# Similarity matmuls of two heads issued by turns on the two halves of TensorE's rows, in a fixed order

## The chip, the core and the metric

The kernel runs on one core of one Trainium2 chip. The time is device microseconds of one execution of the whole program. Three runs of the kernel before took 3486.24, 3478.69 and 3476.59 us; their median is 3478.69.

The names in the text: TensorE (PE in the profile; PEld is its loading of weights) multiplies matrices into PSUM banks, VectorE (DVE), ScalarE (ACT) and GpSimd (POOL) work on elements, SyncE (SP) issues the transfers. Each engine takes its instructions in the order in which they stand in its own queue.

## What is computed

The reference is a small transformer on x of 4 batch elements, 2048 tokens and 256 features, all in float32. Cut to what matters:

```python
x = x + LN(attention_ref(LN(x)))      # softmax(x x^T) over all tokens, times x
x = x + LN(ffn_ref(LN(x)))            # two layers, below

def layer(x):                          # DEPTH = 2, HEADS = 8, DIM_HEAD = 64, WINDOW = 128
    h = shift_token(x)
    q, k, v = split(h @ wqkv)          # to heads
    q, k = rotary_xpos(l2norm(q) * qs, l2norm(k) * ksc)
    # each window of 128 queries sees its own 128 keys and the 128 of the window before
    sim = einsum('bhwid,bhwjd->bhwij', q * 8, k);  mask
    o = softmax(sim) @ v
    x = x + o @ wo
    h = LN(shift_token(x)) @ w1 + b1
    a, g = split(h)
    return x + (a * gelu(g)) @ w2 + b2
```

## The kernel before

Tokens lie on the 128 partitions for the row statistics and the residual stream, features for the products. First comes the attention over all tokens, for each of four batch elements (the first 690 us or so). Then two layers run over 4 x 16 windows of 128 tokens each, 128 window steps in all, with one layer's weights held in SBUF.

**Products in two parts.** A float32 operand is kept as two float32r parts whose sum is exact (`Split`: hi and lo). A product is three matmuls into the same PSUM tile: lo times hi, hi times lo, hi times hi. They are written by the helper `products` (matmul on L149), so nearly all matmuls of the profile carry line 149 and are told apart by tile.

**Similarities (L696 on, function `similarities`).** A window step makes its similarities in two batches (gq 0 and 1) of four heads. A head has 64 features, so its matmul uses 64 of the array's 128 rows. Heads lie in pairs: of a pair, one head (r = 0) has its features on partitions 0 to 63, the other (r = 1) on 64 to 127. The heads of one r share a PSUM tile, `ps[r]`, in a bank of its own; the pair is c = 0 or 1. So a batch has 2 (c) x 2 (r) groups of three matmuls, each of 256 columns (the keys of two windows; 128 in the first window of a batch element). In the profile they are `sim<-kT_h,qT_l`, `sim<-kT_l,qT_h` and `sim<-kT_h,qT_h`.

**What reads them.** For each of the four heads VectorE adds the mask, scales, and finds the row's minimum (L702, `pr<-sim`, with `nm`, by a second small instruction on the same line); ScalarE takes the exponential and its sum (L707); VectorE inverts the four sums (L713, `rr`); GpSimd divides three of the four heads and ScalarE one (L720, L718). Then TensorE transposes (L730, `pp`), the two parts `pT` are made by ScalarE (L132) and VectorE (L137), and the values' matmuls (`po`) and the output's (`pw`) follow.

**Banks.** PSUM tiles come from tags with a fixed number of banks. The tag `sim` has two, shared by `sim`, `pa` (the first product of the feed-forward), `phn` (its transposed input) and `pv` (the values' projection):

```python
BANKS = {'sim': (2, ('sim', 'pa', 'phn', 'pv')), 'po': (3, ('po', 'pw')), 't75': (1, ('pf', 'ph', 'pqk')), ...}
```

**What sets the order.** The window steps' stages (queries and keys, softmax, outputs, feed-forward) are written down by turns after the strings in `TURNS`. What decides the order in each engine's queue is a scheduler: `schedule_with_timeline_sim=True` lets it place the instructions by a simulated time of its own, within what data and buffers allow. In the order that it made, 125 of the 256 batches have the six matmuls of r = 0 and the six of r = 1 as two blocks with other work between them, 121 have the two blocks one directly after the other, and ten (first windows) have other forms.

Of the kernel before, what the change touches and what calls it, by code (L numbers as in the profile page):

```python
# [14 lines left out]
P = 128  # L15
HEADS = 8
DH = 64
# [29 lines left out]
class Split:  # L47
    """A float32 operand in two float32r parts whose sum is exact: its upper 12 bits and the rest."""
# [9 lines left out]
def sandwich_kernel(  # L58
# [16 lines left out]
    """x += LN(attention over the batch's tokens of LN(x)); x += LN(two local-attention layers of LN(x)).  # L75

    First the attention over all tokens for each batch element, then each layer for all of them,
    with that layer's weights in SBUF. Tokens are on the partitions for the row statistics and the
    residual stream, features for the products, which are taken of operands in two parts each.
    """  # L80
    nc = tc.nc
# [3 lines left out]
    HID = w2.shape[1]  # L85
# [3 lines left out]
    NC = HID // P  # whole chunks of the hidden layer  # L89
    TAIL = HID - NC * P  # and the rest, the gate's at partition 64  # L90
    GT = 64
    # Where rows of the tail lie again: to, from, how many.
    PIECES = ((TAIL + 1, 0, GT - TAIL - 1), (GT + TAIL, GT - TAIL - 1, P - 1 - GT - TAIL))
    RING = 3  # windows whose keys and values are kept
# [6 lines left out]
    # ---------------------------------------------------------------- constants  # L101
# [6 lines left out]
    one = const.tile([P, 1], F32, name="one")  # L108
    nc.gpsimd.memset(one, 1.0)
    # Query i of a window sees keys i .. i + 128 of the previous and its own window: those of the  # L110
    # previous from i on, those of its own up to i. Here for the order previous, own, previous.
# [12 lines left out]
    # ---------------------------------------------------------------- operands in two parts  # L124
# [17 lines left out]
    def products(dst, terms, whole=()):  # L142
        """dst = the sum of the terms' lhsT.T @ rhs, with all of float32's bits, and of whole's as they are."""
        todo = []
        for a, b in terms:
            todo += [(a.lo, b.hi), (a.hi, b.lo), (a.hi, b.hi)]
        todo += whole
        for n, (a, b) in enumerate(todo):
            nc.tensor.matmul(dst, a, b, start=(n == 0), stop=(n == len(todo) - 1))  # L149

    # ---------------------------------------------------------------- row statistics
    def statistics(parts, n, name):
        """Mean and variance of n rows' parts, and 1/sqrt(variance + eps): [P, n, 2], [P, n]."""
        k = len(parts[0])
        mv = small.tile([P, 4, 2], F32, tag="mv", bufs=12, name=f"mv_{name}")
        for i in range(n):
            bs = small.tile([P, 2, 6], F32, tag="bs", name=f"bs_{name}_{i}")
            for c, part in enumerate(parts[i]):
                nc.vector.bn_stats(bs[:, c, :], part)
            nc.vector.bn_aggr(mv[:, i, :], bs[:, 0:k, :].rearrange("p c s -> p (c s)"))  # L160
        ve = small.tile([P, 4], F32, tag="ve", name=f"ve_{name}")
        nc.vector.tensor_scalar_add(ve[:, 0:n], mv[:, 0:n, 1], EPS)
        rstd = small.tile([P, 4], F32, tag="rstd", bufs=12, name=f"rstd_{name}")
        nc.gpsimd.tensor_tensor(rstd[:, 0:n], ve[:, 0:n], neghalf[:, 0:n], ALU.pow)
        return mv, rstd
# [6 lines left out]
    def normalize_all(dst, src, mv, rstd, engines, name):  # L172
        """Rows i of src, normalized, on the vector engine or the scalar engine."""
        n = len(src)
        if "a" in "".join(engines):
            mr = small.tile([P, 4], F32, tag="mr", name=f"mr_{name}")
            nc.vector.scalar_tensor_tensor(mr[:, 0:n], mv[:, 0:n, 0], -1.0, rstd[:, 0:n], ALU.mult, ALU.mult)
        for i in range(n):
            for d, s, e in zip(dst[i], src[i], engines[i]):
                if e == "a":  # L180
                    nc.scalar.activation(d, s, AF.Identity, bias=mr[:, i : i + 1], scale=rstd[:, i : i + 1])
                else:
                    normalize(d, s, mv, rstd, i)
# [10 lines left out]
    def add_context(xg, y, b, g):  # L194
        """x + LN(y) goes to DRAM, and y becomes LN of that."""
# [10 lines left out]
    # ---------------------------------------------------------------- attention over all tokens  # L206
    JG = 2

    def global_phase(early, res, keep, big, bank):
        """Attention over all tokens.  # L210

        It stops before the last group's scores, when it's done with early, and after them, when
        it's done with res; the rest, in steps, uses only keep and bank.
        """
# [3 lines left out]
        def slot(tag, n, last):  # L218
            """The pool and the tag for the n-th of a kind of tiles; last are those that the last group uses."""
            n, last = n % GB[tag], [i % GB[tag] for i in last]  # L220
            return (res if n in last else early), f"{tag}{n}"

        def load_x(b, g):
            pool, tag = slot("x", b * NG + g, [B * NG - 1])
            t = pool.tile([P, 4, D], F32, tag=tag, bufs=1, name=f"x_{b}_{g}")
            # The first to come is waited for.
# [6 lines left out]
        def prepare(b, g):  # L233
            """LN(x) of 512 tokens with the features on the partitions."""
            xg = xt[b, g]
            mv, rstd = statistics([[xg[:, s, :]] for s in range(4)], 4, f"x_{b}_{g}")
            # |LN(x_j)|^2, the shift of column j's exponents: the exponents are 64 at most, one is 0.
# [21 lines left out]
        def scores(b, jg, hf):  # L259
            """exp of a half of the rows of JG chunks of scores."""  # L260
# [12 lines left out]
            for j in range(jg * JG, (jg + 1) * JG):  # L273
# [6 lines left out]
                # The scores are symmetric: those of the groups before are transposed here.  # L280
# [27 lines left out]
            for j in range(jg * JG, (jg + 1) * JG):  # L308
                # The sums belong to the contraction's index, so they divide LN(x).
# [14 lines left out]
        def context(b, jg, hf):  # L324
            """Adds the context of JG chunks; at the end x + LN(context) and LN of that go to DRAM."""
            for g in (2 * hf, 2 * hf + 1):
# [19 lines left out]
                if jg == NW // JG - 1:  # L346
                    if b + 1 < B:
                        add_context(early.tile([P, 4, D], F32, tag="xr", bufs=GB["xr"], name=f"xr_{b}_{g}"), y, b, g)
                    # The last one's rest is done when the first layer takes it.
# [37 lines left out]
    # ---------------------------------------------------------------- weights of a layer  # L387
# [5 lines left out]
    def tables(early, pool, l):  # L393
        """Rotation tables with the scales of q and k; the halves are swapped as the rotation does."""
# [29 lines left out]
    # The weights' parts, as they lie in SBUF.  # L424
# [11 lines left out]
    def split_weights(pool, bank, l):  # L436
        """Leaves layer l's weights in two parts in DRAM, piece by piece; each is left half a turn to arrive."""
        # The scale of the layer norm goes into w1, its shift into the bias.
# [34 lines left out]
        for i, (kind, ks, cols, src) in enumerate(pieces):  # L473
# [14 lines left out]
            # The lower part takes raw's place.  # L488
# [18 lines left out]
        # The tail's parts and the bias's, which meet rows of ones, share the rows of one product.  # L507
# [13 lines left out]
    def load_weights(pool, w, l, kinds):  # L521
        """Layer l's weights into w, as soon as the ones before aren't used any more."""
# [8 lines left out]
    # ---------------------------------------------------------------- the layers  # L531
    def layer_phase(pool, bank, ending):
# [22 lines left out]
        def features(l, b, u):  # L555
            """h of windows 2u and 2u + 1, features on the partitions: the second half comes one token late."""
# [21 lines left out]
        def queries_keys(l, b, w, n, wt, own):  # L578
            """Queries, keys and values of window w, left in own; in stages."""
# [19 lines left out]
            # Rotation, with the decay, the scales and, for q, the factor -8 in the tables; l2norm.  # L599
# [46 lines left out]
            # The similarities are scaled by q's.  # L646
# [18 lines left out]
        def local_attention(l, b, w, wt, before, own):  # L665
            """Window w sees itself and the window before it; y += its attention. In two streams of stages."""
# [5 lines left out]
            else:  # L672
# [3 lines left out]
                # In the order of their slots.  # L676
# [7 lines left out]
            def similarities(gq):  # L684
                # Negated similarities; the two heads of a pair use the two halves of the array's
                # rows, and so two banks.
                ps = [bank(f"sim_{at}_{gq}_{r}").rearrange("p (c j) -> p c j", c=2) for r in range(2)]
                for c in range(2):
                    for r in range(2):
# [5 lines left out]
                        products(ps[r][:, c, 0:NK], [(qT[rows_, 2 * gq + c, :], keys)])  # L695
# [28 lines left out]
            def weights(m):  # L724
                """The weights of pair m with the keys on the partitions."""
# [8 lines left out]
            def values(m, pT, po):  # L734
                # Both heads' values against both heads' weights: the diagonal blocks count.
# [42 lines left out]
        def feed_forward(l, b, w0, m, wt):  # L778
            """y += FFN of m windows from w0 on, in stages; h2's first row is there already."""
# [3 lines left out]
            # The second half of the features, one token late.  # L783
# [34 lines left out]
            for n, c in enumerate((*range(TAILPOS), NC, *range(TAILPOS, NC))):  # L818
# [4 lines left out]
                # a * gelu(g) takes the place of a.  # L823
# [54 lines left out]
        def finish(b, w0, m, ys):  # L878
            """x += LN(y) of m windows."""
# [78 lines left out]
    class Pools:  # L958
        """The layers' memory: what the first steps use, to the left, and the rest, once the phase before is over."""
# [4 lines left out]
        def more(self, n):  # L964
            """The part of the phase before goes, what takes its place comes."""
# [46 lines left out]
def _rope(n, window):  # L1012
    """Rotation tables [cos or sin, n, q or k, DH / 2] with xpos's decay, and q's factor 8, negated."""
# [43 lines left out]
```

## Time and profile before

| | |
|---|---|
| median of three runs | 3478.69 us (3476.59 to 3486.24) |
| the profiled execution's span | 3480.2 us |
| granted TensorE clock, mean | 0.991 |
| TensorE matmuls, busy | 3374.0 us (97%), 24312 instructions |
| VectorE busy | 2932.9 us (84%) |
| ScalarE busy | 2495.6 us (72%) |
| GpSimd busy | 1933.8 us (56%) |
| similarity matmuls | 3 x 1024, of them 3 x 960 with 256 columns |

The profiled execution has no other time of its own than its span, which lies within the spread of the three runs. A matmul's length in the profile is from its start to its modelled end, and matmuls overlap: 256 columns are shown as some 280 ns while the next one starts some 120 ns after. So busy time of TensorE is more than the work it has room for, and the step from one start to the next is what a matmul costs. In the timeline a row with "x2" merges two instructions of one kind that overlap.

### The profile page before, as it was taken

How to read it: one execution, taken by the hardware profiler on the slowest of the kernel's cores; microseconds unless marked ns; L12 is line 12 of the kernel's file. 1: busy time of each engine (PE TensorE's matmuls, PEld its weight loads, DVE VectorE, ACT ScalarE, POOL GpSimd, SP SyncE). 2: the span in 40 equal slices, each digit the busy share in tenths (PEclk: the TensorE clock that was granted, in tenths of full speed). 3: DMA queues.
4: the chain of work that ended last, by engine and by line, in shares of the span. 5: the costliest groups of instructions: out<-in, count | busy, mean ns of one | idle time of the engine just before them, and what ended most of it. 6: DMA issues, size and time to landing. Idle time of an engine off the chain costs nothing.

```text
span 3480.2 us, 67843 instructions
## 1 busy us (share of the span) xinstructions
PE 3374.0 (97%) x24312; PEld 3069.6 (88%) x24312; DVE 2932.9 (84%) x7549; ACT 2495.6 (72%) x5826; POOL 1933.8 (56%) x1975
## 2 busy tenths in 40 slices
PE   8999999999999999999999999999999999999997
PEld 7989999978889999999888898888888888888886
DVE  6797877778888888888999888888888888888886
ACT  5556655467777888777777777777777777777774
POOL 3234313265556666666666655666666666566562
PEclk9999999999999999999999999999999999999998
DMA  3243312110000000001111112101000010011001
GB/s 98 93 145 116 127 47 92 63 65 22 23 23 25 24 25 23 23 25 34 36 35 35 49 59 68 29 29 30 29 29 29 29 31 25 26 30 30 29 22 30
DMA packets 158194, 156.70 MB, mean 45 GB/s; under 512 B 27466, under 2 KB 145056, under 8 KB 157344
## 3 DMA queue, kind: packets, MB, share of 16 engines
q1 hardware_dynamic: 157856, 152.36, 14.1%
q8 instruction: 192, 3.15, 0.4%
q14 instruction: 146, 1.20, 0.1%
HBM read 86.39 MB, written 54.79 MB: 41 GB/s over the span
## 4 chain that ended last, share of the span: by engine, by line
PE 79%; DVE 11%; ACT 5%; DMA 2%; issue 2%; POOL 1%; SPq 0%; POOLq 0%; ACTq 0%; DVEq 0%
PE pa L149 12%; PE sim L149 10%; PE po L149 9%; PE pqk L149 9%; PE c L149 8%; PE pf L149 6%; PE pp L730 6%; PE pv L149 5%; PE pw L149 5%; PE s L149 5%; PE pqkT L657 3%; DVE pr L702 2%; DVE hn L168 1%; DVE y L168 1%; DVE qk L648 1%
## 5 line engine op out<-in xcount | busy, mean ns | idle before, releaser
L720 POOL TENSOR_SCALAR pr<-pr,rr 128x256 f32<-128x256 f32 (+1 forms) x768 | 356.1, 481 | 650.9 <-DVE rr L713 494.2
L707 ACT ACTIVATE pr<-pr,nm 128x256 f32<-128x256 f32 (+1 forms) x1024 | 507.8, 498 | 123.4 <-DVE nm L702 118.5
L702 DVE CUSTOM_DVE_ANT_0 pr<-sim,mask,rn 128x256 f32<-128x256 f32 (+1 forms) x1024 | 440.1, 470 | 92.3 <-PE sim L149 88.5
L149 PE MATMUL pa<-hnT_h,w_l 128*128 128x256 f32 x1408 | 407.1, 289 | 3.5 <-DVE hnT_l L137 2.2
L630 POOL TENSOR_TENSOR rn<-ss,neghalf 128x16 f32<-128x16 f32 x128 | 394.1, 3079 | 27.7 <-DVE ss L610 20.0
L616 POOL TENSOR_TENSOR sw<-qk,ab 128x512 f32<-128x512 f32 x256 | 338.3, 1322 | 115.2 <-ACT qk L596 115.2
L149 PE MATMUL pa<-hnT_l,w_h 128*128 128x256 f32 x1408 | 398.8, 283 | 0.3 <-DVE hnT_l L137 0.2
L149 PE MATMUL pa<-hnT_h,w_h 128*128 128x256 f32 x1408 | 399.0, 283 | 0.0
L137 DVE TENSOR_TENSOR pT_l<-pp,pT_h 128x512 fp32r<-128x512 f32 (+1 forms) x512 | 340.0, 664 | 27.7 <-ACT pT_h L132 23.4
L623 POOL TENSOR_TENSOR qk<-qk,ab 128x512 f32<-128x512 f32 x256 | 349.4, 1377 | 10.2 <-ACT sq L602 9.0
L132 ACT CAST pT_h<-pp 128x512 fp32r<-128x512 f32 (+1 forms) x512 | 291.7, 570 | 68.2 <-PE pp L730 62.8
L149 PE MATMUL po<-pT_l,v_h 128*128 128x256 f32 x992 | 316.3, 319 | 4.6 <-DVE pT_l L137 4.6
L730 PE MATMUL pp<-ident,pr 128*128 128x128 f32 x1984 | 314.6, 276 | 3.7 <-DVE pT_l L137 1.7
L149 PE MATMUL po<-pT_h,v_l 128*128 128x256 f32 x992 | 298.2, 301 | 2.6 <-ACT pT_h L132 2.4
L132 ACT CAST act_h<-af 128x256 fp32r<-128x256 f32 x320 | 130.2, 407 | 237.2 <-DVE af L833 233.9
L149 PE MATMUL sim<-kT_h,qT_l 64*128 64x256 f32 (+1 forms) x1024 | 294.0, 329 | 0.9 <-ACT kT_h L132 0.6
L149 PE MATMUL c<-xs_h,e_l 128*128 128x256 f32 x1024 | 285.3, 285 | 3.6 <-ACT y L132 2.5
L149 PE MATMUL c<-xs_l,e_h 128*128 128x256 f32 x1024 | 287.5, 283 | 0.8 <-POOL xs_l L137 0.8
L149 PE MATMUL c<-xs_h,e_h 128*128 128x256 f32 x1024 | 287.5, 283 | 0.0
L149 PE MATMUL po<-pT_h,v_h 128*128 128x256 f32 x992 | 278.9, 281 | 0.0
L149 PEld LDWEIGHTS pa<-hnT_h,w_l 128*128 128x128 f32 x1408 | 269.4, 191 | 5.6 <-DVE hnT_l L137 2.7
L149 PEld LDWEIGHTS pa<-hnT_l,w_h 128*128 128x128 f32 x1408 | 269.5, 191 | 1.1 <-DVE hnT_l L137 1.0
(179 smaller groups left out, 11841.3 us busy)
## 6 DMA issues: line engine op xcount, KB each, us to landing
yd<-y SPq DMA_DIRECT2D x32, 512.0 KB
y<-yd SPq DMA_DIRECT2D x32, 512.0 KB
ab<-abd SPq DMA_DIRECT2D x128, 128.0 KB
x<-in_L_attn_x_dram SPq DMA_DIRECT2D x15, 512.0 KB
x<-x1d SPq DMA_DIRECT2D x15, 512.0 KB
out_dram<-y SPq DMA_DIRECT2D x15, 512.0 KB
h<-y SPq DMA_DIRECT2D x64, 112.0 KB
xr<-in_L_attn_x_dram SPq DMA_DIRECT2D x12, 512.0 KB
```

The costliest lines, as they stand in the source:

```text
L132: (nc.scalar.copy if eng == "a" else nc.vector.tensor_copy if eng == "v" else nc.gpsimd.tensor_copy)(dst, src)
L137: eng.tensor_tensor(dst.lo, src, dst.hi.bitcast(F32), ALU.subtract)
L149: nc.tensor.matmul(dst, a, b, start=(n == 0), stop=(n == len(todo) - 1))
L168: nc.vector.tensor_scalar(dst, src, mv[:, i, 0:1], rstd[:, i : i + 1], ALU.subtract, ALU.mult)
L616: nc.gpsimd.tensor_mul(sw4[:, hs], qk4[:, hs, ::-1, :], ab[:, 1, j].unsqueeze(1).to_broadcast([P, HEADS, 2, DH // 2]),)
L623: (nc.vector if T1[j] == "v" else nc.gpsimd).tensor_mul(qk[:, hs, :], qk[:, hs, :], ab[:, 0, j].rearrange("p h i -> p (h i)").unsqueeze(1) ...
L630: nc.gpsimd.tensor_tensor(rn, ss, neghalf, ALU.pow)
L657: nc.tensor.transpose(pt[:, c * P : (c + 1) * P], qk[:, j * HEADS + 2 * c : j * HEADS + 2 * c + 2, :].rearrange("p h d -> p (h d)"), ident,)
L702: nc.vector.tensor_tensor_reduce(out=pr[:, r, 0:NK], in0=sim, in1=mask[:, m0 : m0 + NK], scalar=3.0e38, scale=own["rn"][:, h : h + 1] if Q ...
L707: nc.scalar.activation(pr[:, r, 0:NK], pr[:, r, 0:NK], AF.Exp, bias=nms[h], scale=-1.0, accum_out=rs[:, h : h + 1],)
L720: (nc.gpsimd if e == "p" else nc.vector).tensor_scalar(pr, pr, rr[:, h : h + 1], 1.0, ALU.mult, ALU.mult)
L730: nc.tensor.transpose(pp[:, f, r, :], prs[m][:, r, f * P : (f + 1) * P], ident)
```

## The change

The four groups of a batch are no longer written one after the other. For each pair c, the three matmuls of r = 1 and the three of r = 0 are written by turns, beginning with r = 1, and a new helper ties each of the twelve to the one before it, without a semaphore (`NoSync`), so that the scheduler keeps them in that order on TensorE's queue. It may still put other instructions between them. The operands, the PSUM tiles and what reads them are the same; only comments and docstrings go besides, which moves the line numbers (`products`' matmul is L161 after, the similarities' own matmul L715).

```diff
+    def in_turn(instructions):
+        for a, b in zip(instructions, instructions[1:]):
+            tc.add_manual_dep(
+                b.ins, a.ins.name,
+                mybir.DependencyInfo(mybir.DependencyClass.NoSync, mybir.DependencyReason.DATA), reason="turns",
+            )
+
+    def terms_of(terms):
         todo = []
         for a, b in terms:
             todo += [(a.lo, b.hi), (a.hi, b.lo), (a.hi, b.hi)]
-        todo += whole
+        return todo
+
+    def products(dst, terms, whole=()):
+        todo = terms_of(terms) + list(whole)
         for n, (a, b) in enumerate(todo):
             nc.tensor.matmul(dst, a, b, start=(n == 0), stop=(n == len(todo) - 1))
...
                 ps = [bank(f"sim_{at}_{gq}_{r}").rearrange("p (c j) -> p c j", c=2) for r in range(2)]
+                queue = []
                 for c in range(2):
-                    for r in range(2):
+                    pair = []
+                    for r in (1, 0):
                         rows_ = slice(r * DH, (r + 1) * DH)
                         keys = Split(*(
                             t[rows_, first : first + (nh - 1) * step + 1 : step, 2 * gq + c, :]
                             for t in (kT.hi, kT.lo)
                         ))
-                        products(ps[r][:, c, 0:NK], [(qT[rows_, 2 * gq + c, :], keys)])
+                        pair.append((ps[r][:, c, 0:NK], terms_of([(qT[rows_, 2 * gq + c, :], keys)])))
+                    for n in range(3):
+                        for dst, todo in pair:
+                            queue.append(nc.tensor.matmul(dst, *todo[n], start=(n == 0), stop=(n == 2)))
+                in_turn(queue)
```

More of the change, by code (lines that the diff above doesn't have):

```diff
@@ L140, in move @@
         queue.dma_start(out=dst.bitcast(F32), in_=src.bitcast(F32) if src.dtype == F32R else src)
-    def products(dst, terms, whole=()):
+    def in_turn(instructions):
[5 more added lines that the diff above has]
+    def terms_of(terms):
         todo = []
```

## The prediction

> **What bounds the kernel now.** I read the page's busy times first, then its chain of work that ended last, then the busy time by stretches of the span, then the timeline of TensorE around the matmuls that the change touches, and last the waits.
>
> ```profile
> span 3480.2 us, 67843 instructions
> PE 3374.0 (97%) x24312; PEld 3069.6 (88%) x24312; DVE 2932.9 (84%) x7549; ACT 2495.6 (72%) x5826; POOL 1933.8 (56%) x1975
> PE 79%; DVE 11%; ACT 5%; DMA 2%; issue 2%; POOL 1%; SPq 0%; POOLq 0%; ACTq 0%; DVEq 0%
> ```
>
> TensorE is busy nearly always and carries 79% of the chain; VectorE is next with 84% and 11%. The stretches say how close VectorE is in the layers, which start at about 700 us:
>
> ```profile
> core 0: us, PE busy (x) PEld busy (x) DVE busy (x) ACT busy (x) POOL busy (x), PEclk, DMA share, GB/s
> 2100.00:2500.00 400.00, 387.81 (x2806) 350.57 (x2805) 350.11 (x924) 301.25 (x742) 248.60 (x258) 0.99 0.10 28
> ```
>
> In 400 us VectorE is idle for 50. A busy TensorE is not one at its peak, so I count steps from one matmul's start to the next. In the timeline (start, length, engine, line, operation) a matmul of 256 columns takes a step of 0.12 us although each is shown 0.28 long. Here is a half of a batch of similarities alone (six matmuls on 64 rows):
>
> ```profile
> 2000.14 0.28 PE L149 MATMUL po<-pT_l,v_h 128*128 128x256 f32 x1
> 2000.26 0.28 PE L149 MATMUL po<-pT_h,v_h 128*128 128x256 f32 x1
> 2000.47 0.38 PE L149 MATMUL sim<-kT_h,qT_l 64*128 64x256 f32 x1
> 2000.69 0.28 PE L149 MATMUL sim<-kT_l,qT_h 64*128 64x256 f32 x1
> 2000.81 0.28 PE L149 MATMUL sim<-kT_h,qT_h 64*128 64x256 f32 x1
> ...
> 2001.16 0.27 PE L149 MATMUL sim<-kT_h,qT_h 64*128 64x256 f32 x1
> 2001.37 0.38 PE L149 MATMUL pw<-wo_h,oT_l 128*128 128x256 f32 x1
> ```
>
> Entering costs a step of 0.21 instead of 0.12, the first step inside 0.22, leaving 0.21: the half takes 0.90 from its first start to the next kind's, and 0.99 with the 0.09 lost on entry. And here are two halves, the lower rows' six and then the upper rows' six, directly one after the other:
>
> ```profile
> 2006.89 0.38 PE L149 MATMUL sim<-kT_h,qT_l 64*128 64x256 f32 x1
> 2007.12 0.28 PE L149 MATMUL sim<-kT_l,qT_h 64*128 64x256 f32 x1
> 2007.23 0.28 PE L149 MATMUL sim<-kT_h,qT_h 64*128 64x256 f32 x1
> 2007.24 0.39 PE L149 MATMUL sim<-kT_h,qT_l 64*128 64x256 f32 x2
> 2007.46 0.29 PE L149 MATMUL sim<-kT_l,qT_h 64*128 64x256 f32 x2
> 2007.58 0.28 PE L149 MATMUL sim<-kT_h,qT_h 64*128 64x256 f32 x2
> 2007.70 0.28 PE L149 MATMUL sim<-kT_h,qT_l 64*128 64x256 f32 x1
> ...
> 2007.94 0.28 PE L149 MATMUL sim<-kT_h,qT_h 64*128 64x256 f32 x1
> 2008.15 0.66 PE L730 MATMUL pp<-ident,pr 128*128 128x128 f32 x4
> ```
>
> The rows with x2 are the point: two matmuls, one of each half, start within 0.01 us and the next pair follows 0.12 later. So the two halves of the array do run side by side here, but only three of six pairs: twelve matmuls take 1.26 us, 1.35 with the entry.
>
> **The change part by part.** *Order.* Each of the 256 batches (128 window steps, two each) has 12 similarity matmuls. In the order of the program before, 125 batches stand as two separate halves, 121 as twelve together (six more, of a first window with 128 columns, alternate by three already, and four have 2 and 10). In the changed program 141 stand as twelve alternating, 105 as one lone matmul of the upper rows, then other work, then the eleven others; the ten of first windows remain about as they were. No instruction is added or removed on any engine, and the 839 transfers of the SP queue are the same ones. The scheduler does shift everything else, on POOL's and SP's queues too; I give that no price beyond the waits below, as POOL idles 38% and the transfers use 10% of the DMA engines in the stretch shown.
>
> *TensorE's steps, removed.* Before: 125 x 2 x 0.99 = 247.5 and 121 x 1.35 = 163.4, together 410.9 us. After, if all six pairs run as the three x2 rows do: 0.22 + 4 x 0.12 + 0.21 + 0.09 on entry = 1.00 for a block. A lone matmul pays entry and exit for itself: 0.09 plus a step between 0.21 (an exit) and 0.31 (an exit and the slow first step), so 0.30 to 0.40; I take 0.35, between, as no row shows one. After: 141 x 1.00 + 105 x 1.35 = 282.8. That is 128 us less (123 to 133), all of it on the engine that carries the chain.
>
> *Waits, added.* PE's queue is in order, and less TensorE time now lies between a result and its use. For each matmul that waits for another engine I counted the TensorE steps between it and the last matmul that its data depend on. With under 2.5 us of cover there are 386 such waits before and 784 after. In the trace of before a wait with 1.5 to 2.5 us of cover costs about 0.1 us on average (mostly the next weight load, which comes late), one with 1.0 to 1.5 us about 0.25. Taking each class at its mean in before: about 40 us more. Ends: nothing, if VectorE simply idles less, and 80 us, if each of the 398 new ones cost 0.2. I take 45, a little over the middle, because VectorE has less idle time left to take them up.
>
> *The banks.* A batch now holds both banks of the tag sim until VectorE has read four tiles, 4 x (470 + 83 ns) = 2.2 us with line 702's two groups; pa, phn and pv use the same two banks. Before, VectorE could start on one half when its six were done; now its first reading waits for the whole batch, 0.9 us after the batch starts, as long as a half took alone. That is no loss where the twelve stand together. In the 105 split batches the lower rows' reading starts later by the work in between (some 2 to 4 us); the rows that use it, the transposes of L730, stand a median of 10 us behind in both orders, which covers it.
>
> *VectorE as the next limit.* Its work stays. Its waits for ScalarE in the layers (rr 60, af 40, and splits qT, pT, oT, ss, act, hT, kT of 13 to 25 each, in all 227 us of 2780) are 33 in 400 us, so 350 + 33 = 383 is a floor of about 17 us less per 400, or 118 us over the layers. The gain of 128 can't come through whole.
> The Trainium skill (TensorEngine Tiling (Array Packing), "PSUM Bottleneck") speaks against the change here: tiling makes TensorE faster, not the reading of PSUM, which may become the bottleneck. By this rule alone the sum would be the 118 us just worked out, or nothing if VectorE's idle time stayed at 50; by the matmul rows alone 128. No row before decides between them.
>
> *Sum.* 3480.2 - 128 + 45 = 3397; I say 3400. The sum is made against the profiled execution, whose span is 1.5 us over the median of the runs shown, 3478.69, less than their own spread of 10; 0.3% (10 us) is about what a measurement can tell from no change.
>
> **The rivals.** *A: VectorE takes over.* TensorE's steps go, but VectorE's idle time falls only from 50 to 45 in 400: 35 us gained, 3445. For it: VectorE's 88% in the layers and its waits for ScalarE. Against it: 88.5 us of its idle time are waits for the similarities themselves, and those ought to shrink.
>
> ```profile
> DVE pr L702 <- PE sim L149: 88.5, 142, 2.0
> PE phn L811 <- DVE nm L702: 30.8, 16, 2.4
> ```
>
> *B: slower, the bank wait.* The second line is TensorE standing until VectorE has read a batch out of a bank: 16 times, 1.93 us each. Both banks are now wanted at once, in a fixed order beginning with the upper rows, and all that follows in PE's queue stands behind that wait. Once 43 of the 256 batches pay 1.93 us (83 us, 128 less the 45), the gain is gone; at 60 it is 3513. Against it: the next matmul on a batch's bank stands a median of 2.8 us of steps after the batch (2.7 is what an end and four readings need), close, but at most places not short by a whole wait.
>
> *C: the change doesn't do what it says.* If the pairs don't keep up over six (loads of both halves getting in each other's way), a block costs 1.35 as now: 141 x 1.35 + 105 x 1.70 = 368.9, 42 us less, and with the 45 of waits 3483, no change. The x2 rows speak against it: the weight loads of both halves went side by side there too.
>
> *D: all of it.* Waits stay as they are: 3352.
>
> **How the numbers follow.** Forecast (3375 to 3435) 0.50; D (below 3375) 0.12; A (3435 to 3470) 0.20; C or a draw (3470 to 3490) 0.05; B (above 3490) 0.13. Faster 0.82, same 0.05, slower 0.13. The range is 3358 to 3472, leaving out about 0.05 below and 0.15 above.
>
> **What would show it.** Right: pairs of sim matmuls (x2) 0.12 us apart through whole blocks, about 0.9 us a block; a smaller share of sim in the chain; VectorE near 360 busy of 400. Wrong by A: a larger DVE share of the chain with idle TensorE spread over many short waits. Wrong by B: one group, PE sim, phn, pv or pa waiting for DVE nm, with 100 us and more. Wrong by C: rows of sim with x1.

## The result and the profile after

The changed kernel takes 3544.77 us, the median of four runs (3537.96 to 3546.88), against 3481.27 us for the kernel before (3476.59 to 3486.24): a ratio of 1.0178, with a 95% interval of 1.0163 to 1.0192. It is slower by 1.8%, where 3400 us and faster had been forecast. The profiled run took 3537.96 us with a span of 3536.2, that is 56 us more than the span before.

The page of the kernel after, its span, its busy times and its chain of work that ended last:

```profile
span 3536.2 us, 67828 instructions
PE 3321.2 (94%) x24312; PEld 2968.3 (84%) x24312; DVE 3029.2 (86%) x7549; ACT 2478.9 (70%) x5826; POOL 1918.2 (54%) x1975
PE 48%; DVE 29%; ACT 14%; DMA 3%; issue 3%; POOL 2%; SPq 1%; POOLq 0%; DVEq 0%; ACTq 0%
```

Three things differ from before. TensorE is busy for 53 us less, with the same 24312 matmuls, and yet the span is longer: so it stands idle for 109 us more (215 against 106). Its share of the chain fell from 79% to 48%, and VectorE's rose from 11% to 29%, ScalarE's from 5% to 14%. And VectorE is busy for 96 us more although it has the same 7549 instructions, which nothing in the change had asked for.

The same stretch as before, by its busy times:

```profile
core 0: us, PE busy (x) PEld busy (x) DVE busy (x) ACT busy (x) POOL busy (x), PEclk, DMA share, GB/s
2100.00:2500.00 400.00, 375.94 (x2787) 332.37 (x2786) 356.55 (x905) 294.02 (x737) 240.09 (x253) 0.99 0.13 41
```

VectorE went from 350 to 357 busy of 400, TensorE from 388 to 376. The granted clock of this stretch is the same 0.99.

Over the whole span the clock has a small share. The trace shows short episodes, mostly of 3.4 us, at half clock. In the kernel before one of them comes 1.4 us behind a TensorE wait of 2.4 us (phn for nm, ended at 2545.65); it and the 3.4 us behind it:

```profile
2547.00:2550.40 3.40, 3.40 (x9) 2.68 (x9) 3.34 (x9) 1.57 (x4) 2.27 (x1) 0.50 0.00 0
2551.00:2554.40 3.40, 3.40 (x31) 3.40 (x30) 2.29 (x4) 3.38 (x6) 3.40 (x6) 1.00 0.00 0
```

Inside, matmuls of 512 columns take steps of 0.43 us, just ahead of it 0.23. There are 13 such episodes before (61 us) and 19 after (82 us). TensorE's steps in the layers that fall into them take 19 us over the usual ones of their kind before and 29 after, so at most 10 of the 56 us are the clock's. What sets an episode off was not tested; 11 of the 13 and 17 of the 19 begin within 5 us of the end of a TensorE step longer than 1 us.

The change itself does what it says. The timeline of TensorE in the kernel after (start, length, engine, line, operation) shows a batch of twelve:

```profile
2011.72 0.28 PE L161 MATMUL pf<-w2t,tail 128*128 128x256 f32 x1
2011.93 0.38 PE L715 MATMUL sim<-kT_h,qT_l 64*128 64x256 f32 x2
2012.15 0.28 PE L715 MATMUL sim<-kT_l,qT_h 64*128 64x256 f32 x2
2012.27 0.28 PE L715 MATMUL sim<-kT_h,qT_h 64*128 64x256 f32 x2
2012.39 0.28 PE L715 MATMUL sim<-kT_h,qT_l 64*128 64x256 f32 x2
2012.51 0.28 PE L715 MATMUL sim<-kT_l,qT_h 64*128 64x256 f32 x2
2012.63 0.28 PE L715 MATMUL sim<-kT_h,qT_h 64*128 64x256 f32 x2
```

All six similarity rows are pairs (x2), 0.12 us apart after the slow first step. Over the whole trace such a block takes a median of 0.909 us from its first start to the next kind's (1.254 before). Where one matmul of the upper rows stands alone, it costs this:

```profile
2017.25 0.38 PE L715 MATMUL sim<-kT_h,qT_l 64*128 64x256 f32 x1
2017.56 0.50 PE L161 MATMUL pqk<-wq_h,hT_l 128*128 128x512 f32 x1
```

0.31 us from start to start, with the 0.09 lost on entry 0.40.

I added up all steps of TensorE in the layers (from 700 us on) from start to start, and split off what a step has over the usual one of its kind as a wait. Before: 2492 us of steps and 261 of waits. After: 2377 and 431. So 115 us of steps went, and 170 us of waits came: 55 more, which is the 56 of the span. (Steps slowed by the clock count as waits here. The split moves by some 15 us with what is called the usual step; the sum does not.) The waits are many and short: those over 0.35 us rose from some 80 or 90 to some 220. By the matmul that waits (count, us): phn 17 (41) to 52 (67), pp 7 (5) to 35 (34), po 8 (8.5) to 32 (27), pv 3 (3.5) to 19 (17), sim 2 (0.9) to 19 (17).

TensorE's larger waits in the kernel after (who waits, for whom, us in total, times, the longest in us):

```profile
PE pp L751 <- DVE pT_l L137: 27.9, 31, 2.3
PE phn L832 <- DVE nm L723: 27.4, 22, 2.9
PE po L161 <- ACT pT_h L132: 20.4, 32, 1.2
PE sim L715 <- DVE nm L723: 15.8, 21, 0.9
PE phn L832 <- ACT hn L193: 15.6, 12, 7.4
...
PE phn L832 <- DVE hn L180: 14.4, 18, 1.1
PE pqkT L669 <- DVE qk L657: 13.3, 17, 1.6
PE pv L161 <- DVE nm L723: 12.4, 16, 1.3
```

No single group carries the loss. Before, the phn wait for nm was the only one above 10 us. The waits of VectorE for the similarities, 88.5 us before, did shrink, to 11.0 (26 waits); but VectorE spent that time on longer instructions and on other waits (its wait for h's transfer grew from 11.2 to 53.9 us).

### The profile page after: what moved, and what is told of

The parts are those of the page before. It is cut to its first block, busy times and chain, and to the rows that moved or that the text cites. A ratio compares the mean times of both kernels' runs of the same rounds, so it can differ in the third digit from the quotient of the medians.

```text
span 3536.2 us, 67828 instructions
## 1 busy us (share of the span) xinstructions
PE 3321.2 (94%) x24312; PEld 2968.3 (84%) x24312; DVE 3029.2 (86%) x7549; ACT 2478.9 (70%) x5826; POOL 1918.2 (54%) x1975
## 4 chain that ended last, share of the span: by engine, by line
PE 48%; DVE 29%; ACT 14%; DMA 3%; issue 3%; POOL 2%; SPq 1%; POOLq 0%; DVEq 0%; ACTq 0%
PE pa L161 9%; PE c L161 9%; PE po L161 5%; DVE pr L723 5%; PE s L161 5%; ACT pr L728 4%; PE pf L161 4%; DVE hn L180 3%; PE pp L751 3%; DMA h<-y 3%; PE pw L161 3%; PE pqk L161 2%; PE pqkT L669 2%; PE sim L715 2%; DVE pT_l L137 2%
## 5 line engine op out<-in xcount | busy, mean ns | idle before, releaser
L723 DVE CUSTOM_DVE_ANT_0 pr<-sim,mask,rn 128x256 f32<-128x256 f32 (+1 forms) x1024 | 423.3, 467 | 14.3 <-PE sim L715 11.0
L628 POOL TENSOR_TENSOR sw<-qk,ab 128x512 f32<-128x512 f32 x256 | 346.4, 1354 | 152.2 <-ACT qk L608 149.4
L161 PE MATMUL pa<-hnT_h,w_l 128*128 128x256 f32 x1408 | 411.8, 292 | 7.8 <-DVE hnT_l L137 6.5
L642 POOL TENSOR_TENSOR rn<-ss,neghalf 128x16 f32<-128x16 f32 x128 | 386.1, 3016 | 36.4 <-DVE rr L734 31.1
L161 PE MATMUL pa<-hnT_l,w_h 128*128 128x256 f32 x1408 | 398.6, 283 | 0.5 <-DVE hnT_l L137 0.3
L161 PE MATMUL pa<-hnT_h,w_h 128*128 128x256 f32 x1408 | 398.6, 283 | 0.0
L635 POOL TENSOR_TENSOR qk<-qk,ab 128x512 f32<-128x512 f32 x256 | 336.0, 1327 | 3.1 <-ACT sq L614 2.9
L161 PE MATMUL po<-pT_h,v_l 128*128 128x256 f32 x992 | 298.0, 300 | 20.9 <-ACT pT_h L132 20.4
L161 PE MATMUL po<-pT_l,v_h 128*128 128x256 f32 x992 | 316.7, 319 | 0.8 <-DVE pT_l L137 0.7
L161 PE MATMUL c<-xs_l,e_h 128*128 128x256 f32 x1024 | 287.5, 283 | 0.8 <-POOL xs_l L137 0.8
L161 PE MATMUL c<-xs_h,e_l 128*128 128x256 f32 x1024 | 285.2, 285 | 3.0 <-ACT y L132 2.3
L161 PE MATMUL c<-xs_h,e_h 128*128 128x256 f32 x1024 | 287.5, 283 | 0.0
L161 PE MATMUL po<-pT_h,v_h 128*128 128x256 f32 x992 | 282.6, 285 | 0.0
L161 PEld LDWEIGHTS pa<-hnT_h,w_l 128*128 128x128 f32 x1408 | 268.6, 191 | 15.5 <-DVE hnT_l L137 11.1
L751 PEld LDWEIGHTS pp<-ident,pr 128*128 128x128 f32 x1984 | 231.0, 141 | 57.9 <-POOL qk L657 12.3
L161 PEld LDWEIGHTS pa<-hnT_l,w_h 128*128 128x128 f32 x1408 | 269.0, 191 | 1.3 <-DVE hnT_l L137 1.1
```

The source lines that it names most:

```text
L628: nc.gpsimd.tensor_mul(sw4[:, hs], qk4[:, hs, ::-1, :], ab[:, 1, j].unsqueeze(1).to_broadcast([P, HEADS, 2, DH // 2]),)
L635: (nc.vector if T1[j] == "v" else nc.gpsimd).tensor_mul(qk[:, hs, :], qk[:, hs, :], ab[:, 0, j].rearrange("p h i -> p (h i)").unsqueeze(1) ...
L642: nc.gpsimd.tensor_tensor(rn, ss, neghalf, ALU.pow)
L723: nc.vector.tensor_tensor_reduce(out=pr[:, r, 0:NK], in0=sim, in1=mask[:, m0 : m0 + NK], scalar=3.0e38, scale=own["rn"][:, h : h + 1] if Q ...
L751: nc.tensor.transpose(pp[:, f, r, :], prs[m][:, r, f * P : (f + 1) * P], ident)
```

## The experiments

Four questions are open after this comparison: is it the turns or the order that the scheduler made around them; is it the tie or the row order; is it VectorE; and which property of the new order costs the time. All ratios are to the kernel before, run on the same chip beside each experiment, with 95% intervals; its medians there were 3482 to 3484 us.

**Turns without a new order, and the new order without turns.** Both kernels edit only TensorE's queue after the scheduler is done, in the places where similarity matmuls stand directly together. The rest of the program, on all engines, stays in its order.

In before's order the 121 batches of six and six are taken by turns, lower rows first; in after's order the turns of its 246 batches (141 of twelve together, 105 of eleven beside a lone one) are put back to half after half, upper rows first. The calls, and what the helper does with each run of similarity matmuls (u is a matmul with its weight load, a and z are those of the half that begins and of the other):

```diff
         sandwich_kernel(tc, *args)
+    _again(nc, True)
...
         sandwich_kernel(tc, *args)
+    _again(nc, False)
...
+        if alternate and pat == "000000111111":
+            new = [u for p in zip(a, z) for u in p]
+        elif not alternate and pat == "101010101010" or pat == "01010101010" and not alternate:
+            new = a + z if len(a) == 6 and len(z) == 6 else z + a
```

> The order of every engine is that of the kernel before; only in the 121 places where the two halves' six matmuls stand directly one after the other they are put by turns, lower rows first. Theory S (the alternation itself is good, the loss comes from the new order that the tie made the scheduler choose): 121 x 0.35 = 42 us less, some 10 of it lost to waits, so about 3450 us (3435 to 3465). Theory V (VectorE is so near its limit that TensorE's steps are worth little): 3465 to 3482. Theory H (two halves by turns disturb the chip, for instance the readings of PSUM): over 3482.

> The order of every engine is that of the changed kernel; only where its similarity matmuls stand by turns they are put half after half again, the six (or five) of the upper rows first. Theory S: TensorE's steps grow by 246 x 0.35 = 86 us; if the order has made VectorE the limit, only part of it shows: 3565 to 3630 us, above the changed kernel's 3545. Theory H: 3545 or less.

Turns in before's order: 3468.85 us, ratio 0.996 (0.9947 to 0.9973), faster than both kernels. Halves in after's order: 3561.06 us, 1.0231 (1.0214 to 1.0248). The four together:

| us | halves | turns | steps, halves to turns | waits |
|---|---|---|---|---|
| order of before | 3482 | 3469 | 2492 to 2446 | 261 to 278 |
| order of after | 3561 | 3545 | 2458 to 2377 | 385 to 431 |

The turns gain 13 us in the one order and 16 in the other. The new order costs 79 us with halves and 76 with turns. So the turns are good for a little and the scheduler's new order is what makes the kernel slow. Also, of the 45 and 81 us of steps that the turns take out, only 13 and 16 come through; added waits of 17 and 46 take most of the others. (The sums do not close for halves in after's order: its steps and waits are 90 us above before's, its span 79, so that row's split is some 10 us too high.) Neither time fell into the range of theory S, which had the turns worth more: 3469 lies 4 us above its 3465, where theory V had it, and 3561 lies 4 us under its 3565. The page and the same stretch with turns in before's order:

```profile
span 3454.6 us, 67843 instructions
PE 75%; DVE 13%; ACT 7%; issue 2%; DMA 1%; POOL 1%; SPq 0%; POOLq 0%; DVEq 0%; ACTq 0%
```

```profile
2100.00:2500.00 400.00, 386.48 (x2834) 348.67 (x2834) 348.56 (x911) 300.54 (x736) 248.72 (x256) 0.99 0.09 27
```

The shares are those of before, nearly, and so is VectorE's 349 of 400. (This profiled run was the shortest of eight, 12.5 us under the median, and its mean clock of 0.993 the highest; the others had 0.989 to 0.992.)

**The tie.** The twelve stay tied to one another, but half after half, the lower rows first, as the kernel before had them.

```diff
-                queue = []
+                queue, pairs_ = [], []
...
-                    for r in (1, 0):
+                    for r in (0, 1):
...
-                    for n in range(3):
-                        for dst, todo in pair:
+                    pairs_.append(pair)
+                for r in range(2):
+                    for pair in pairs_:
+                        dst, todo = pair[r]
+                        for n in range(3):
```

And the opposite: turns as changed, with the tie left out, so that the scheduler may place each of the twelve as it likes.

```diff
-                in_turn(queue)
```

> A tie as in the changed kernel, but the order tied is half after half, lower rows first, as most batches stood before: 125 batches in two separate halves and 127 together, the readings 593 of 768 in a row. Theories U and G both: like the kernel before, 3460 to 3500 us; if the tie itself does harm: over 3520.

> The changed kernel without the tie: the matmuls are written by turns, but the scheduler is free. It puts nearly all back half after half: 148 batches as two halves together, 99 as two separate halves, as before though upper rows first. Theory S: near the kernel before, 3460 to 3500 us: what the tie does to the order is the loss. If the loss came from the upper rows going first or from chance alone in the scheduler's choices, 3510 to 3550.

Tied halves: 3482.5 us, 0.9995 (0.9985 to 1.0004), and waits of 264 us: the tie alone costs nothing. Without the tie: 3602.88 us, 1.0348 (1.0333 to 1.0364), slower still and outside both ranges that were expected; the scheduler then put them half after half again, the upper rows first, 148 batches together and 99 in two places. So what is left of the change as a suspect is the order of the rows in the batch, and that it comes by turns.

**Which rows come first.** VectorE's readings and ScalarE's exponentials take the heads of a pair with r = 0 first. The kernel before fills r = 0 first too; the changed one fills r = 1 first. Three kernels, one line each: turns with r = 0 first; turns as changed but read with r = 1 first; and the kernel before with r = 1 filled first, without turns and without tie.

```diff
-                    for r in (1, 0):
+                    for r in (0, 1):
                         rows_ = slice(r * DH, (r + 1) * DH)
```

```diff
                     prs.append(pr)
-                    for r in range(2):
+                    for r in (1, 0):
                         h = 4 * gq + 2 * c + r
```

```diff
                 for c in range(2):
-                    for r in range(2):
+                    for r in (1, 0):
                         rows_ = slice(r * DH, (r + 1) * DH)
```

> The changed kernel with the tie and the turns, but each turn begins with the lower rows' matmul (r = 0) in place of the upper rows'. VectorE still has nearly all of its four readings of a batch in a row (743 of 768 neighbours, 760 in the changed kernel, 595 before). Theory U (what costs is that the upper rows are filled first while VectorE reads the lower rows first): about 3440 to 3480 us. Theory G (what costs is that a batch comes whole, so that VectorE's four readings stand in one block): like the changed kernel, 3530 to 3560.

> The changed kernel, with VectorE's and ScalarE's loop over the two halves turned too, so that the upper rows are both filled and read first. Readings in a row: 743 of 768. Theory U: the loss goes, 3440 to 3480 us. Theory G: 3530 to 3560.

> The kernel before with one edit: the loop over the two halves runs over (1, 0), so the upper rows' matmuls are written first; no turns, no tie. VectorE's readings stand in a row in 741 of 768. Theory U: all of the loss of the freely scheduled version, about 3600 us. Theory G: also slower, as the readings stand in a row, 3540 to 3610. If neither: 3470 to 3500.

| | filled first | read first | us | ratio |
|---|---|---|---|---|
| before | lower | lower | 3484 | 1 |
| before, r = 1 filled first | upper | lower | 3603.23 | 1.0345 (1.0329 to 1.036) |
| turns (after) | upper | lower | 3544.77 | 1.0178 (1.0163 to 1.0192) |
| turns | lower | lower | 3498.06 | 1.0043 (1.0027 to 1.006) |
| turns | upper | upper | 3496.7 | 1.0038 (1.0023 to 1.0053) |

Filling in the order in which the batch is read, in either direction, takes 47 or 48 us off the changed kernel; filling against it puts 119 us on the kernel before, which has no turn at all. Both expectations missed the first two: 3497 and 3498 lie between theory U's 3480 and theory G's 3530, so the row order is a part of the loss and not all of it. Each of these edits also made the scheduler plan anew. TensorE's waits for VectorE's reading and for the lower part of pT with turns, lower rows first:

```profile
PE pp L751 <- DVE pT_l L137: 43.2, 35, 2.4
PE pv L161 <- DVE nm L723: 18.0, 22, 2.0
...
PE sim L715 <- DVE nm L723: 8.5, 12, 1.1
...
PE phn L832 <- DVE nm L723: 5.3, 9, 1.6
```

The three waits for nm, in which TensorE stands until a bank has been read, come to 31.8 us here and to 55.6 in the kernel after (27.4 + 15.8 + 12.4). So half of the 47 us is seen directly in the bank waits; the other half lies in the other groups, which all moved with the order (in pp for pT_l even upwards). In the kernel before with the upper rows filled first, the largest wait of TensorE is of another kind again:

```profile
PE pqkT L657 <- DVE qk L645: 47.9, 16, 4.8
```

Here the rotated queries and keys are late, an operation that does not touch the similarities' banks. So the re-planned order is at work, not the banks alone.

Even the better two stay 28 to 29 us behind the turns put into before's order (3497 and 3498 against 3469), with 61 us fewer steps on TensorE (2385 against 2446) and 104 us more waits (382 against 278). A part of these waits is the clock's: TensorE's steps at half clock take 35 us over the usual with turns, lower rows first, and 14 with turns in before's order. That is up to 21 of the 40 us between these two profiled spans, and less of the 28 or 29 between the medians, since the profiled run in before's order had an unusually high clock. The chain with turns, lower rows first:

```profile
PE 42%; DVE 32%; ACT 16%; DMA 4%; issue 3%; POOL 2%; SPq 0%; POOLq 0%; DVEq 0%; ACTq 0%
```

**VectorE's load.** If VectorE is the limit, work taken off it should help after and do little before. The floor of the squared sums, max(ss, 1e-24), is replaced by ss + 1e-24 on ScalarE, in both kernels.

```diff
+    tiny = const.tile([P, 1], F32, name="tiny")
+    nc.gpsimd.memset(tiny, 1e-24)
...
-            nc.vector.tensor_scalar_max(ss, ss, 1e-24)
+            nc.scalar.activation(ss, ss, AF.Identity, bias=tiny, scale=1.0)
```

> The changed kernel with another 78 us of VectorE's work taken to ScalarE: the small maximum on the sums of squares (ss, 128 instructions) becomes an addition of 1e-24 there. Theory V (VectorE's load is what the changed kernel runs against): 30 to 70 us less than the changed kernel, 3475 to 3515. Theory L (hn's place alone matters): 3530 to 3550.

> The same edit on the kernel before: 91 us of VectorE's work go, of which 57 are stretch. Theory V: TensorE is the limit there, so 0 to 20 us less, 3460 to 3485.

After, it takes 3570.46 us, 1.0253 (1.0238 to 1.0268), although VectorE's busy time did fall from 3029 to 2961 us. Before, it takes 3484.0, 1.000 (0.9989 to 1.0012). Less work for VectorE and 26 us more time: the forecast of 3475 to 3515 fell, and theory L's 3530 to 3550 as well. It does not clear VectorE, though, for the new plan brought more than the edit: the mean clock fell from 0.989 to 0.982 in the profiled runs, with 32 episodes at half clock (129 us) against 19 (82 us). TensorE's steps in them take 48 us over the usual, against 29; that is up to 19 us of the 33 between the two spans.

**Where hn is made.** TensorE's wait for hn (the normalized rows that phn transposes) was among the larger groups. Of its four parts ScalarE makes one and VectorE three; here ScalarE makes all four.

```diff
-HN = 'avvv'
+HN = 'aaaa'
```

> The changed kernel with the feed-forward's layer norm (hn) made wholly by ScalarE: 192 instructions leave VectorE, where they took 150 us in the changed kernel, 86 of it stretch while GpSimd ran. Theory L (the changed order puts hn behind VectorE's readings and beside GpSimd's long rotations, and TensorE's phn waits for it, 67 us in 52 long waits): 60 to 100 us less than the changed kernel, 3445 to 3485. If hn only happens to be where a general shortage shows: 3510 to 3545.

> The same edit on the kernel before, as its control: hn takes 98 us of VectorE there, 33 of it stretch, and TensorE carries the chain. Theory L: within 25 us of the kernel before, 3455 to 3500, so that the changed kernel gains at least 40 us more from it than this one.

After: 3597.26 us, 1.0331 (1.0314 to 1.0348). Before: 3522.24, 1.0117 (1.0102 to 1.0132). The edit costs 53 us after and 40 before, where the theory had a gain in the first; it fell, and 3597 lies outside the other range too (3510 to 3545), as 3522 does outside the control's (3455 to 3500).

**A prediction from the waits' cover.** The waits of the kernels so far went with the number of places where a matmul has less than 1.5 us of TensorE steps between what it needs and itself: 100 before, 195 after, 191 with turns lower first, 124 and 139 in the two with TensorE's queue alone edited, 96 with tied halves. Putting all four parts of hn on VectorE gave orders with other counts (115 before, 138 with turns lower first, 213 after), so it could be tried as a forecast. The first hunk is made in all three, the second in the first kernel alone.

```diff
-HN = 'avvv'
+HN = 'vvvv'
...
-                    for r in (1, 0):
+                    for r in (0, 1):
```

> The turns with the lower rows first, tied, and the feed-forward's layer norm (hn) made wholly by VectorE: 64 instructions more there, none of hn on ScalarE. Places with under 1.5 us of cover: 138, against 191 with ScalarE's share. Theory C (cover): waits of TensorE grow by about 1.75 us for each such place in the runs so far, so some 90 us fewer than the 382 of the lower-first version, and 3410 to 3460 us. Theory V (VectorE's load): slower than the lower-first version's 3498, 3500 to 3560.

> The same move of hn to VectorE on the kernel before, as the control: 115 places with under 1.5 us of cover, against 100. Theory C: 26 us of waits more, 3490 to 3525. Theory V: TensorE is the limit there, 3480 to 3500.

> The same move on the changed kernel (upper rows first): 213 places, against 195. Theory C: 30 us more than the changed kernel, 3555 to 3600. Theory V: also slower, by the 64 instructions' 0.34 to 1.3 us, 3560 to 3600; this one tells little between the two, but would break C if it were faster.

Turns lower first: 3508.54 us, 1.007 (1.0055 to 1.0085). Before: 3540.93, 1.0161 (1.0144 to 1.0178). After: 3547.57, 1.0181 (1.0166 to 1.0196). The forecasts by cover missed all three, two of them with too low a time, by 15 us and more, and one with too high a time. The rival, VectorE's load, had the first in its range (3500 to 3560) and missed the other two. Counting cover went with the waits afterwards, but did not forecast a time. Two things can be read from it all the same. Among these three, filling against the reading costs 39 us (3548 against 3509), so that effect does not hang on one order. And with hn on VectorE the turns lower first are 32 us faster than the same edit of the kernel before (3509 against 3541): turns with a new order may come out on either side.

What stays open: which property of the new order costs the 28 or 29 us that remain when filling and reading agree, beyond the clock's part. In the scheduler's orders with turns VectorE does its four readings of a batch more often in a row (743 of 768 neighbouring pairs, 595 before), since no reading can begin until the whole batch is done. But the kernel before with the upper rows filled first has 741 without any turn and takes 3603, and the kernel before with hn on VectorE has about as few as the kernel before (573 against 589, counted in the traces) and is slow as well (3541), so this alone does not decide. It could not be tested at a fixed order, because every edit off TensorE's queue made the scheduler plan all of it anew.

## Why the prediction was wrong

**The pairs run side by side: right.** Blocks of 0.909 us against 0.91 worked out; the lone matmul cost 0.40, the top of the 0.30 to 0.40 (0.35 taken). Steps fell by 115 us where 128 had been summed; the lone matmul, 105 times 0.05 us, is 5 of the 13. (Of the three x2 rows that the prediction read, the first merges starts 0.12 us apart and not 0.01; three pairs do start within 0.01 us, so the count of three of six stands.) Rival C, that the pairs don't keep up, is out.

**Waits, added: wrong, and this is the step that failed.** 45 us were taken, with ends of 0 and 80; it was 170. With steps and waits as measured the sum is 3480.2 - 115 + 170 = 3535, the span that came (3536.2). The reason behind the wrong size is a line further up: "The scheduler does shift everything else ... I give that no price beyond the waits below". The count of covers (386 to 784 waits under 2.5 us) did say that the order had become tighter, but each was priced at its mean in the trace of before; that there was slack behind most of them there, which the new order lacks, is my reading and not shown wait by wait. The two kernels with TensorE's queue alone edited show the price at fixed matmuls: 76 to 79 us for the new order, which by itself is some 115 us of waits (385 less 261, less the 10 by which that sum does not close). Up to 10 of the 170 are steps at half clock, which the prediction did not have either.

**The banks, "That is no loss": wrong, in part.** The 10 us between the reading and the transposes were looked at; who comes next on the bank was looked at in rival B alone (2.8 us of steps where 2.7 are needed) and got no price in the sum. In the kernel after, the rows that are filled first are read last. Filling in the order of reading takes 47 to 48 us off, the new plan of each such kernel included. The bank waits named in the prediction grew from 33.6 us (30.8 + 2.8) to 55.6, so rival B's mechanism is there with 22 us; its price of 83 us from one group did not come about, and its time (3513) was still 32 us under the result. It was the only rival on the right side.

**VectorE as the next limit: the sign right, the mechanism incomplete.** The chain and the stretch look like rival A: VectorE at 29% of the chain, TensorE idle in many short waits. The time does not (3445). VectorE's own work was taken as fixed; it grew by 96 us through the order alone (2935 us with turns in before's order and 3032 with halves in after's, against 2933 before and 3029 after; more below). That VectorE's growth caused the loss is not shown: the runs that took work off it were slower. The Trainium skill (TensorEngine Tiling (Array Packing), "PSUM Bottleneck") says that tiling speeds up TensorE and not the reading of PSUM, which may become the limit after a fourfold speedup; here two halves run side by side. VectorE's readings of the similarities took 470 ns before and 467 after, and its waits for them fell from 88.5 to 11.0 us, so VectorE has become the later one of the two. But that is mostly the order: turns alone, in before's order, leave 79.7 us of these waits, and the new order with halves has 29.3. The rule gives no size, and the 76 us of the order is not its subject.

**The chances.** Slower had 0.13, all of it on one mechanism. The range (3358 to 3472) left out the 3483 of C and the 3513 of B, and no price in it was for the re-planning, which in these runs moved a kernel by up to 119 us with a single swapped loop.

## What to carry to other kernels

Where a scheduler decides the order, the price of an edit is the edit plus a new plan, and the plan can be the larger part: here 13 to 16 us gained and 76 to 79 lost. Freeze the order and make the edit in place to see what it is worth by itself; in this case that version was also the fastest of all, 3469 us. Where two banks are filled and read in turn, fill them in the order in which they are read (39 to 48 us in three comparisons here, each with a new plan), and price new tight waits above their old mean: at little more than that mean they came to 45 us here, and 170 were measured.

## What the runs showed of the hardware

**Small instructions of VectorE on SBUF can last as long as those of GpSimd beside them.** Groups of VectorE by line, before and after (operation, shapes, count, busy us and mean ns); first before (what stands behind the second bar is the idle time ahead of them):

```profile
L168 DVE TENSOR_SCALAR hn<-h,mv_f,rstd_f 128x128 f32<-128x128 f32 x128 | 63.9, 499 | 0.0
...
L162 DVE TENSOR_SCALAR ve_f<-mv_f 128x2 f32<-128x2 f32 x64 | 16.0, 250 | 1.6
...
L177 DVE SCALAR_TENSOR_TENSOR mr_f<-mv_f,rstd_f 128x2 f32<-128x2 f32 x64 | 15.4, 241 | 1.7 <-POOL rstd_f L164 1.4
```

and the same three after:

```profile
L180 DVE TENSOR_SCALAR hn<-h,mv_f,rstd_f 128x128 f32<-128x128 f32 x128 | 102.4, 800 | 0.0
...
L189 DVE SCALAR_TENSOR_TENSOR mr_f<-mv_f,rstd_f 128x2 f32<-128x2 f32 x64 | 38.7, 605 | 7.7 <-POOL rstd_f L176 7.7
...
L174 DVE TENSOR_SCALAR ve_f<-mv_f 128x2 f32<-128x2 f32 x64 | 35.2, 550 | 1.8
```

These three alone are 81 of the 96 us. The timeline of VectorE in the kernel after shows how one comes about:

```profile
2510.39 0.94 DVE L189 SCALAR_TENSOR_TENSOR mr_f<-mv_f,rstd_f 128x2 f32<-128x2 f32 x1
2511.25 1.39 DVE L180 TENSOR_SCALAR hn<-h,mv_f,rstd_f 128x128 f32<-128x128 f32 x1
2512.57 1.31 DVE L180 TENSOR_SCALAR hn<-y,mv_f,rstd_f 128x128 f32<-128x128 f32 x1
2513.80 0.33 DVE L180 TENSOR_SCALAR hn<-h,mv_f,rstd_f 128x128 f32<-128x128 f32 x1
```

and that of GpSimd over the same time:

```profile
2510.01 2.55 POOL L635 TENSOR_TENSOR qk<-qk,ab 128x512 f32<-128x512 f32 x2
2512.49 1.30 POOL L628 TENSOR_TENSOR sw<-qk,ab 128x512 f32<-128x512 f32 x1
```

The same instruction takes 0.33 us once GpSimd has ended and 1.31 to 1.39 beside it; hn's ends, 2512.64 and 2513.88, lie within 0.1 us of GpSimd's, 2512.56 and 2513.79. The readings of PSUM (L702 before, L723 after) show no such thing, 470 and 467 ns on average. The Trainium skill (SBUF — State Buffer, "Who interferes with whom") has VectorE and GpSimd share a pair of ports that one instruction holds to its end while the other is blocked, and this only for VectorE's faster modes or two SBUF inputs; the rows agree in that the blocked one lasts until the other ends, though it ends too soon after (0.08 us) for all of its 0.33 us to begin only then, and no row shows which of the two conditions hn falls under. What was new to me is how much it adds up to: how much longer VectorE's same instructions last depends on the order alone. Summed over the layers, what they take beyond a short one of their kind (the shortest twentieth) is 273 us before, 392 after, 353 with turns lower first, and 277 with turns in before's order. How much of that is GpSimd's doing was not separated.

**Two halves of the array keep step through a whole batch.** Six pairs of 64-row matmuls follow one another 0.12 us from pair to pair, the rate of one full matmul of 256 columns; entering and leaving the 64-row form costs 0.21 us each in place of 0.12, and the first step 0.22. With six and six in the queue, as in the kernel before, the trace has the second half's first matmul start at 2007.240 and the first half's fourth, which stands ahead of it in the queue, at 2007.357; the prediction's row at 2007.24 merges the two. So over the two halves matmuls did not start strictly in the queue's order here.
